# A transformer block with Strassen products: ScalarE's operations of the QKV stages in written order, and the first stage's weight sums moved from GpSimd to VectorE

## The chip, the cores and the metric

The kernel runs on one core of one Trainium2 chip. The metric is the device time of one execution in microseconds (us). All numbers ahead of the result come from one profiled execution of the kernel before the change, and from three timed runs of it.

## The reference

Two sequences of 2048 tokens with 512 features go through one transformer block that a condition vector modulates. All data is float32. Cut to what matters:

```python
mod = silu(condition) @ Wada + bada
sh_a, sc_a, gt_a, sh_m, sc_m, gt_m = split(mod, 6, axis=1)
xn = layernorm(x, g1, be1)
xm = xn * (1 + sc_a) + sh_a
q, k, v = heads(xm @ Wqkv)                 # 16 heads of 32
x = x + gt_a * (causal_softmax(q @ k.T / sqrt(32)) @ v @ Wproj + bproj)
xm = layernorm(x, g2, be2) * (1 + sc_m) + sh_m
x = x + gt_m * (gelu(xm @ W1 + b1) @ W2 + b2)
```

## The kernel before

The program runs, one after the other: the QKV stage of sequence 0 (about 18 to 220 us of the profile), its attention, a projection stage together with the QKV stage of sequence 1 (about 745 to 1005 us), its attention, a projection stage, and the MLP. This change touches the two QKV stages alone.

**A QKV stage** (class `Qkv`) loops over four groups `g` of 512 tokens. A group has six units: four blocks `f` of 128 features of queries and keys (`keys_and_queries`) and two units of values (`values`). Each unit is a 2x2 block product done in Strassen's manner, with seven products instead of eight, on operands that are sums of blocks of the weights (S1, S3, S2, S4 in the table `SUMS`) and sums of blocks of the tokens. The products go into three PSUM banks, a, b and c. The order in a unit is

```python
step("a", A11, True, first, 0, 0), step("b", S1, True, first, 1, 1),
step("a", S2, False, first, 0, 1), step("b", S4, False, last, 0, 1),
step("c", A12, True, last, 0, 0),  step("a", S3, False, last, 1, 1),
step("a", A22, False, direct, 1, 0),
```

A bank that is used again is not cleared: S2 is accumulated on top of A11 in bank a, after ScalarE has copied what A11 left there (`first`, L963 for queries and keys, L1034 for values). `last` is VectorE's addition of a bank to such a copy (L976, L982, L1038). The seventh product, A22, is put off until two products of the next unit have been issued. In the first unit of sequence 0 (`plain`) eight ordinary products replace the seven.

Queries and keys are split into a rounded part `hi`, which ScalarE makes (L968), and the rest `lo`, which VectorE subtracts in groups 0 and 1 and GpSimd in groups 2 and 3 (L970). Both are stored to DRAM by SyncE's queue (L935), and are loaded again in another layout for the attention (L323, L348). There are three `hi` buffers, so a fourth `hi` waits until the first has been stored.

**Slots.** After each product comes a slot (`tick` with its number n, 42 in a group). It holds the work for the next group and other side work: the load of the next x rows (slot 3, L816), the statistics, 1/std and the first two normalised tiles (slot 14: `stats` L216, `inv_std` L222, `normal` L869), transposing and modulating them (slot 18: `norm`, L272), the second two tiles (slots 24 and 28), token sums (L901), in groups 1 to 3 score products `s` whose maxima VectorE takes (L476, L481), and pieces of weight sums for the MLP, which GpSimd adds (L1153) and stores.

**What sets the order.** Each engine runs its instructions in the order of its own queue and waits at the head of it. An instruction wrapped in `act(...)` (or a matmul, in `mm(...)`) keeps its written place among the others so wrapped on its engine. The place of all others is chosen by a scheduler when the program is built, by its own estimate of when they can run. DMA issues are in such queues too, most of them in SyncE's. Before the change, of the ScalarE operations in the QKV stages, none of those of L222, L272, L869, L963, L968, L1009 and L1034 is wrapped.

**Weight sums.** A weight sum is one elementwise addition or subtraction of two blocks in SBUF. For queries and keys each of the four sums of a feature block is 128x256 elements (`weight_sum`, L841), for values 128x512 (`value_weight_sums`, L846). In the first stage GpSimd makes all twenty of them: blocks 1, 2 and 3 and the values in a row ahead of the stage, and block 0 in slot 7 (block 0 of group 0 is `plain` and needs none).

Of the kernel before, what the change touches and what calls it, by code (L numbers as in the profile page):

```python
# [17 lines left out]
P = 128  # L18
# [9 lines left out]
def dit_block_kernel(  # L28
# [177 lines left out]
    def act(ins):  # L206

        return tc.keep_in_program_order(ins)
# [10 lines left out]
        nc.vector.bn_aggr(mv[:, n, :], st)  # L219

    def inv_std(mv, rstd, shift, lo, hi):
        nc.scalar.activation(rstd[:, lo:hi], mv[:, lo:hi, 1], AF.Sqrt, bias=eps)  # L222
        nc.vector.reciprocal(rstd[:, lo:hi], rstd[:, lo:hi])
        nc.vector.scalar_tensor_tensor(
            shift[:, lo:hi], mv[:, lo:hi, 0], -1.0, rstd[:, lo:hi], ALU.mult, ALU.mult
        )
# [7 lines left out]
    def transposed(pool_, psum, xts, n0, mv, rstd, a, c, b, dst, xns=None, share=False):  # L234

        count = len(xts)
        per = 512 // (count * P)  # L240
        by_act = xns is not None
        xns = xns or []
        for t, xt in enumerate(xts):
            if by_act:
                continue
            xn = pool_.tile([P, D], F32, tag="xn", name="xn", bufs=3)
            n = n0 + t
            nc.vector.tensor_scalar(
                xn, xt, mv[:, n, 0:1], rstd[:, n : n + 1], ALU.subtract, ALU.mult
            )  # L250
            xns.append(xn)
        banks = []
        for cc in range(0, C, per):
            ps = psum.tile([P, per, count * P], F32, tag="mm", name="ps_xt")
            for ci in range(per):
                for t in range(count):
                    transpose(
                        ps[:, ci, t * P : (t + 1) * P],
                        xns[t][:, (cc + ci) * P : (cc + ci + 1) * P],
                    )  # L260
            banks.append(ps)

        def modulate(chunks=range(C)):
            for k in chunks:
                src = banks[k // per][:, k % per, :]
                if k % 2 == 0 and (share or not by_act):
                    nc.vector.tensor_scalar(
                        dst[:, k, :], src,
                        a[:, k, b : b + 1], c[:, k, b : b + 1], ALU.mult, ALU.add,
                    )  # L270
                else:
                    nc.scalar.activation(  # L272
                        dst[:, k, :], src, AF.Identity,
                        bias=c[:, k, b : b + 1], scale=a[:, k, b : b + 1],
                    )

        return modulate
# [518 lines left out]
    class Qkv:  # L796
# [43 lines left out]
            w = self.w  # L840
            act(engine.tensor_tensor(w[:, n, :, f], w[:, x, :, f], w[:, y, :, f], op))  # L841

        def value_weight_sums(self):
            w = self.wv
            for n, x, y, op in SUMS:
                act(nc.gpsimd.tensor_tensor(w[:, n], w[:, x], w[:, y], op))  # L846

        def stats(self, g, t, keep=False):

# [5 lines left out]
        def normal(self, g, j, early=False):  # L855

            b = self.row.b
            if j == 0 and g > b:
                for t in range(MTT):
                    self.stats(g, t)  # L860
            for t in (2 * j, 2 * j + 1):
                n, xt = b * NT + g * MTT + t, self.xts[g][t]
                if early:
                    nc.vector.tensor_scalar(
                        xt, xt, mv1[:, n, 0:1], rstd1[:, n : n + 1],
                        ALU.subtract, ALU.mult,
                    )
                else:
                    nc.scalar.activation(  # L869
                        xt, xt, AF.Identity,  # L870
                        bias=shift1[:, n : n + 1], scale=rstd1[:, n : n + 1],
                    )

        def norm(self, g, j, share=False):
# [70 lines left out]
        def keys_and_queries(self, g, f, hp):  # L945

            ops = self.operands(g)
            los = [self.lo_tile(hp) for _ in range(2)]

            def part(i, j):  # L950
                return los[i].bitcast(F32)[:, j * HALF_T : (j + 1) * HALF_T]

            def product(ps, n, new):
                for k in range(HK):
                    mm(
                        ps, self.w[:, n, k, f * P : (f + 1) * P], ops[n][:, k],
                        start=new and k == 0, stop=k == HK - 1,
                        skip_group_check=not new,
                    )

            def first(ps, i, j):
                scale = HD**-0.5 if i == 0 else 1.0
                nc.scalar.activation(part(i, j), ps, AF.Copy, scale=scale)  # L963

            def split(i):
                hi, lo = self.hi_tile(hp), los[i]
                d = lo.bitcast(F32)
                nc.scalar.copy(hi, d)  # L968
                engine = nc.vector if g < 2 else nc.gpsimd
                engine.tensor_tensor(lo, d, hi.bitcast(F32), ALU.subtract)  # L970
                self.stored(g, f, i, (hi, lo))

            def last(ps, i, j):
                d = part(i, j)
                if i == 0:
                    nc.vector.scalar_tensor_tensor(  # L976
                        d, ps, HD**-0.5, d, ALU.mult, ALU.add
                    )
                    if j == 0:
                        split(0)  # L980
                else:
                    nc.vector.tensor_tensor(d, d, ps, ALU.add)  # L982

            def direct(ps, i, j):
                first(ps, i, j)
                split(1)

            return self.unit(product, first, last, direct)

        def plain(self, g, f, hp):  # L990


            xmT, steps = self.xmT[g], []
            for which in range(2):
                box = []
                for k in range(C):
                    def run(which=which, k=k, box=box):
                        if k == 0:
                            box.append(self.psum.tile([P, MT], F32, tag="mm", name="ps_qk"))
                        n = BASE[2 * which + k // HK][0]  # L1000
                        mm(
                            box[0], self.w[:, n, k % HK, f * P : (f + 1) * P], xmT[:, k, :],
                            start=k == 0, stop=k == C - 1,
                        )
                        if k < C - 1:
                            return
                        hi, lo = self.hi_tile(hp), self.lo_tile(hp)
                        scale = HD**-0.5 if which == 0 else 1.0
                        nc.scalar.activation(hi, box[0], AF.Copy, scale=scale)  # L1009
                        nc.vector.scalar_tensor_tensor(  # L1010
                            lo, box[0], scale, hi.bitcast(F32), ALU.mult, ALU.subtract
                        )
                        self.stored(g, f, which, (hi, lo))
                    steps.append(run)
            return steps

        def values(self, g, t):

            ops, vv = self.operands(g), self.row.vv

            def part(i, j):
                w = D // 2
                return vv[:, g * MTT + 2 * j + t, i * w : (i + 1) * w]

            def product(ps, n, new):
                for k in range(HK):
                    mm(
                        ps, ops[n][:, k, t * P : (t + 1) * P], self.wv[:, n, k],
                        start=new and k == 0, stop=k == HK - 1,
                        skip_group_check=not new,  # L1030
                    )

            def first(ps, i, j):
                nc.scalar.copy(part(i, j), ps)  # L1034

            def last(ps, i, j):
                d = part(i, j)
                nc.vector.tensor_tensor(d, d, ps, ALU.add)  # L1038

            return self.unit(product, first, last, first)  # L1040
# [221 lines left out]
    with pool("wada") as wp, pool("qkv0") as qp, pool("hl0") as hp, pool(  # L1262
# [110 lines left out]
                modulate((k, k + 1))  # L1373
        for n in (S1, S2, A22):
            qkv.token_sum(0, n)
        for f in (1, 2, 3):
            for k in range(4):
                qkv.weight_sum(nc.gpsimd, k, slice(f * P, (f + 1) * P))
        act(nc.vector.tensor_copy(pick, pickc.unsqueeze(3).to_broadcast([P, 2, B, P])))

        def also(g, n):

            if (g, n) == (0, 7):
                for k in range(4):
                    qkv.weight_sum(nc.gpsimd, k, slice(0, P))
            pieces.tick()
            if g == 0 and n == 24:
                load_wada(2, 5)
# [6 lines left out]
                else:  # L1395
                    scale_shift(a2, c2, r_g2, r_be2, 3, 4)

        qkv.value_weight_sums()
        pieces = Pieces()
        spare_k = [row.key_room(q) for q in (2, 3)]  # L1400
        w1p, w2p = HK * P, 7 * P
# [32 lines left out]
    with pool("qkv1") as qp, pool("ps_qkv1", bufs=6, space=PSUM) as ps_mm:  # L1434
# [24 lines left out]
        project_phase(past, ps_mm, between)  # L1459

        def also(g, n):
            if (g, n) == (0, 10):
                qkv.value_weight_sums()
            pieces.tick()

        with pool("hl1") as hp:
# [563 lines left out]
```

## Time and profile before

| | us |
|---|---|
| median of 3 runs (2363.38 to 2366.47) | 2365.2 |
| the profiled execution, its own time | 2364.18 |
| its span in the profile | 2362.5 |
| TensorE (PE) busy in the span | 2316.3 (98%) |
| VectorE (DVE) busy | 1437.2 (61%) |
| ScalarE (ACT) busy | 1005.3 (43%) |
| GpSimd (POOL) busy | 1117.3 (47%) |
| first QKV stage, 18.9 to 240 us: PE busy of 221.1 us | 203.8, mean granted clock 0.95 |
| projection and second QKV stage, 745 to 1010 us: PE busy of 265 us | 258.1, clock 1.00 |
| attention of sequence 0, 240 to 745 us: PE busy of 505 us | 501.1, clock 1.00 |

How to read the profile: PEld is TensorE's loading of weights, which runs beside its products. A name such as ACT L963 is an engine and the kernel's line. In a timeline a row gives the start, the busy time, the engine, the line, the operation, the tiles that it writes and reads with their shapes, the number of like instructions that were merged, and in brackets the idle time of the engine before it with what ended that. "SPq" and "POOLq" are DMA issues in a queue. "PEclk" is the share of TensorE's clock that the chip granted. A wait for several things is put down to the one that came last by the profile's reckoning.

### The profile page before, as it was taken

The page shows a single profiled execution, that of the slowest core. Times are in us where ns is not written, and L with a number is a line of the kernel's source. Part 1 is how long each engine was busy: PE and PEld are TensorE (multiplying, and loading weights), DVE is VectorE, ACT ScalarE, POOL GpSimd, SP SyncE. Part 2 cuts the span into 40 slices and gives each one's busy share as a digit, 9 for nine tenths or more (in the row PEclk, how much of TensorE's full clock was granted, in tenths as well). Part 3 has the DMA queues.
Part 4 walks back from the last instruction along what each step waited for, and adds up shares of the span by engine and source line. Part 5 has one row for each costly group of instructions (what it writes and reads, how often), then busy time and mean ns, then how long its engine had stood idle before and what let it go on. Part 6 is the DMA issues. An engine that isn't in the chain of part 4 may idle for free.

```text
span 2362.5 us, 34358 instructions
## 1 busy us (share of the span) xinstructions
PE 2316.3 (98%) x12067; PEld 1409.6 (60%) x12067; DVE 1437.2 (61%) x2964; ACT 1005.3 (43%) x1948; POOL 1117.3 (47%) x1261
## 2 busy tenths in 40 slices
PE   7999999999999999999999999999999999999998
PEld 5777555555554488855555555444585486487477
DVE  5567666666665666776666666653473374365356
ACT  3333555555556144355555555603322322332320
POOL 4343997878884593179887997460000000000000
PEclk9999999999999999999999999999999999999999
DMA  8887233231132787442323113273254254353433
GB/s 249 270 260 221 50 77 72 71 83 46 57 127 82 261 297 250 143 92 59 82 64 99 32 48 123 78 252 108 93 170 149 91 179 143 116 168 127 136 123 130
DMA packets 160518, 311.64 MB, mean 132 GB/s; under 512 B 16544, under 2 KB 48844, under 8 KB 158552
## 3 DMA queue, kind: packets, MB, share of 16 engines
q1 hardware_dynamic: 155488, 285.53, 39.6%
q0 software_dynamic: 4480, 23.36, 2.6%
q8 instruction: 95, 1.56, 0.3%
q14 instruction: 79, 0.65, 0.1%
q10 hardware_dynamic: 376, 0.55, 0.1%
HBM read 229.95 MB, written 87.29 MB: 134 GB/s over the span
## 4 chain that ended last, share of the span: by engine, by line
PE 90%; DVE 3%; DMA 2%; POOL 2%; issue 1%; ACT 1%; SPq 0%; POOLq 0%; DVEq 0%; ACTq 0%
PE ps_a L204 24%; PE st L204 20%; PE ps_b L204 12%; PE o L204 11%; PE s L204 10%; PE ps_c L204 6%; PE sm L204 4%; PE ps_o L204 2%; PE ps_xt L212 1%; DVE mx L481 1%; POOL ee L634 1%; DVE junk L476 1%; PE ps_o L212 1%; DMA x1d<-xt 0%; DMA x<-in_x_dram 0%
## 5 line engine op out<-in xcount | busy, mean ns | idle before, releaser
L606 ACT ACTIVATE e<-st 128x512 f32<-128x512 f32 (+1 forms) x1152 | 573.9, 579 | 429.7 <-PE st L204 358.0
L634 POOL TENSOR_TENSOR ee<-ee,e 128x512 f32<-128x512 f32 x424 | 529.1, 1286 | 4.4 <-ACT e L606 4.1
L481 DVE TENSOR_REDUCE mx<-s 128x1 f32<-128x512 f32 x604 | 407.6, 687 | 196.3 <-PE s L204 195.0
L204 PE MATMUL s<-kst,qst 128*128 128x512 f32 (+3 forms) x1032 | 418.5, 409 | 11.0 <-DVE mx L481 7.1
L204 PE MATMUL st<-qst,kst 128*128 128x512 f32 (+3 forms) x1280 | 409.4, 387 | 0.0
L204 PE MATMUL ps_a<-sum,w 128*128 128x256 f32 (+1 forms) x1088 | 346.6, 454 | 0.0
L204 PE MATMUL o<-e,vv 128*32 128x512 f32 (+3 forms) x2560 | 300.5, 538 | 1.9 <-POOL e L612 1.9
L204 PEld LDWEIGHTS st<-qst,kst 128*128 128x128 f32 x1280 | 227.4, 188 | 94.2 <-issue 62.0
L476 DVE CUSTOM_DVE_ANT_0 junk<-s,causal 128x512 bf16<-128x512 f32 (+3 forms) x428 | 208.7, 488 | 108.1 <-PE s L204 100.0
L204 PEld LDWEIGHTS ps_a<-sum,w 128*128 128x128 f32 x1088 | 206.3, 190 | 109.8 <-issue 91.4
L204 PEld LDWEIGHTS s<-kst,qst 128*128 128x128 f32 x1032 | 194.7, 189 | 124.1 <-DVE mx L481 59.3
L634 POOL TENSOR_TENSOR ee<-e 128x512 f32<-128x512 f32 x168 | 210.4, 1286 | 103.1 <-ACT e L606 99.3
L612 POOL TENSOR_SCALAR_AFFINE_SELECT e<-e 128x128 f32<-128x128 f32 (+1 forms) x384 | 122.1, 353 | 83.8 <-ACT e L606 81.0
L204 PE MATMUL st<-fold,sel 32*128 32x512 f32 (+1 forms) x1152 | 148.5, 480 | 0.4
L1609 DVE TENSOR_TENSOR h<-c,ps_b 128x512 f32<-128x512 f32 x32 | 22.0, 689 | 202.0 <-PE ps_b L204 202.0
L204 PEld LDWEIGHTS st<-fold,sel 32*128 32x128 f32 x1152 | 59.2, 181 | 143.2 <-ACT e L606 86.6
L204 PEld LDWEIGHTS o<-e,vv 128*32 128x32 f32 x2560 | 61.5, 108 | 101.5 <-issue 79.4
L204 PE MATMUL ps_b<-sum,w 128*128 128x256 f32 (+1 forms) x384 | 120.6, 450 | 0.0
L1783 ACT ACTIVATE h<-h,cols 128x512 f32<-128x512 f32 x96 | 69.3, 722 | 120.4 <-DVE h L1609 120.4
L481 DVE TENSOR_REDUCE mx<-st 128x1 f32<-128x512 f32 x164 | 112.7, 687 | 4.2 <-PE st L204 1.8
L970 POOL TENSOR_TENSOR lo<-lo,hi 128x512 fp32r<-128x512 f32 x32 | 40.6, 1271 | 147.6 <-ACT hi L968 147.5
L204 PEld LDWEIGHTS ps_b<-sum,w 128*128 128x128 f32 x384 | 73.0, 190 | 37.2 <-issue 30.6
(208 smaller groups left out, 3117.6 us busy)
## 6 DMA issues: line engine op xcount, KB each, us to landing
qst<-q SPq DMA_DIRECT2D x128, 256.0 KB
kst<-k SPq DMA_DIRECT2D x128, 256.0 KB
w<-w1d SPq DMA_DIRECT2D x32, 896.0 KB
w<-w2d SPq DMA_DIRECT2D x28, 1024.0 KB
w<-w2d SPq DMA_DIRECT2D x28, 768.0 KB
q<-hi SPq DMA_DIRECT2D x32, 256.0 KB
q<-lo SPq DMA_DIRECT2D x32, 256.0 KB
k<-hi SPq DMA_DIRECT2D x32, 256.0 KB
```

The costliest lines, as they stand in the source:

```text
L204: return tc.keep_in_program_order(nc.tensor.matmul(*args, **kw))
L212: return tc.keep_in_program_order(nc.tensor.transpose(dst, src, ident[:n, :n]))
L476: nc.vector.tensor_tensor_reduce(junk[:, :w], s[:, :w], causal[:, QB - w :], 1.0, MASKED, ALU.add, ALU.max, m,)
L481: nc.vector.tensor_reduce(m, s[:, :w], axis=AX.X, op=ALU.max)
L606: act(nc.scalar.activation(e[:, :w], sts[h][:, :w], AF.Exp))
L612: nc.gpsimd.affine_select(d, d, pattern=[[0, len(tiles)], [1, P]], compare_op=ALU.is_ge, fill=0.0, base=0, channel_multiplier=-1,)
L634: act(engine.tensor_tensor(dst, x, y, ALU.add))
L970: engine.tensor_tensor(lo, d, hi.bitcast(F32), ALU.subtract)
L1609: act(nc.vector.tensor_tensor(dst, x, y, ALU.add))
L1783: nc.scalar.activation(d, ps, AF.Gelu, bias=col(r_b1 + half * HF + f, 1))
```

## The change

All ScalarE operations of the QKV stages are wrapped in `act`, so that they stand in ScalarE's queue in the order in which the code issues them. In the first stage VectorE makes the weight sums: the four of block 1 ahead of the stage, and then one in every other slot from slot 7 on: block 2 in slots 7 to 13, block 3 in 15 to 21, the values in 23 to 29, block 0 in 31 to 37. In the second stage the four value sums stay on GpSimd, but are issued one each in slots 10 to 13 instead of four in slot 10.

```diff
 def inv_std(mv, rstd, shift, lo, hi):
-    nc.scalar.activation(rstd[:, lo:hi], mv[:, lo:hi, 1], AF.Sqrt, bias=eps)
+    act(nc.scalar.activation(rstd[:, lo:hi], mv[:, lo:hi, 1], AF.Sqrt, bias=eps))
...
 # in the same way: modulate (L272), normal (L869), first and split of
 # keys_and_queries (L963, L968), plain (L1009), first of values (L1034)
...
-    def value_weight_sums(self):
+    def value_weight_sum(self, engine, k):
+        n, x, y, op = SUMS[k]
         w = self.wv
-        for n, x, y, op in SUMS:
-            act(nc.gpsimd.tensor_tensor(w[:, n], w[:, x], w[:, y], op))
+        act(engine.tensor_tensor(w[:, n], w[:, x], w[:, y], op))
...
-    for f in (1, 2, 3):
-        for k in range(4):
-            qkv.weight_sum(nc.gpsimd, k, slice(f * P, (f + 1) * P))
+    for k in range(4):
+        qkv.weight_sum(nc.vector, k, slice(P, 2 * P))
...
     def also(g, n):
-        if (g, n) == (0, 7):
-            for k in range(4):
-                qkv.weight_sum(nc.gpsimd, k, slice(0, P))
+        if g == 0 and 7 <= n < 39 and n % 2:
+            part, k = (n - 7) // 8, (n - 7) % 8 // 2
+            if part == 2:
+                qkv.value_weight_sum(nc.vector, k)
+            else:
+                f = (2, 3, None, 0)[part]
+                qkv.weight_sum(nc.vector, k, slice(f * P, (f + 1) * P))
...
-    qkv.value_weight_sums()
...
     def also(g, n):                      # second stage
-        if (g, n) == (0, 10):
-            qkv.value_weight_sums()
+        if g == 0 and 10 <= n < 14:
+            qkv.value_weight_sum(nc.gpsimd, n - 10)
```

More of the change, by code (lines that the diff above doesn't have):

```diff
@@ L271, in modulate @@
                 else:
-                    nc.scalar.activation(
-                        dst[:, k, :], src, AF.Identity,
-                        bias=c[:, k, b : b + 1], scale=a[:, k, b : b + 1],
+                    act(
+                        nc.scalar.activation(
+                            dst[:, k, :], src, AF.Identity,
+                            bias=c[:, k, b : b + 1], scale=a[:, k, b : b + 1],
+                        )
                     )
@@ L868, in normal @@
                 else:
-                    nc.scalar.activation(
-                        xt, xt, AF.Identity,
-                        bias=shift1[:, n : n + 1], scale=rstd1[:, n : n + 1],
+                    act(
+                        nc.scalar.activation(
+                            xt, xt, AF.Identity,
+                            bias=shift1[:, n : n + 1], scale=rstd1[:, n : n + 1],
+                        )
                     )
@@ L962, in first @@
                 scale = HD**-0.5 if i == 0 else 1.0
-                nc.scalar.activation(part(i, j), ps, AF.Copy, scale=scale)
+                act(nc.scalar.activation(part(i, j), ps, AF.Copy, scale=scale))
             def split(i):
@@ L967, in split @@
                 d = lo.bitcast(F32)
-                nc.scalar.copy(hi, d)
+                act(nc.scalar.copy(hi, d))
                 engine = nc.vector if g < 2 else nc.gpsimd
@@ L1008, in run @@
                         scale = HD**-0.5 if which == 0 else 1.0
-                        nc.scalar.activation(hi, box[0], AF.Copy, scale=scale)
+                        act(nc.scalar.activation(hi, box[0], AF.Copy, scale=scale))
                         nc.vector.scalar_tensor_tensor(
@@ L1033, in first @@
             def first(ps, i, j):
-                nc.scalar.copy(part(i, j), ps)
+                act(nc.scalar.copy(part(i, j), ps))
             def last(ps, i, j):
```

## The prediction

> **What bounds the kernel now.** I read the table by windows first, to see where TensorE is not busy. The change touches the two QKV stages only, and the built programs show TensorE's order to be the same before and after; so what can be won is TensorE's idle time there, and its time at a low clock. Columns: window, length, busy time of PE, PEld, DVE, ACT, POOL, then granted clock, DMA share, GB/s.
>
> ```profile
> 20.00:40.00 20.00, 11.52 (x32) 6.93 (x31) 13.49 (x17) 6.93 (x12) 18.46 (x23) 0.77 0.66 210
> 40.00:60.00 20.00, 20.00 (x100) 17.63 (x100) 6.40 (x13) 10.53 (x26) 3.72 (x3) 0.98 0.87 238
> 80.00:100.00 20.00, 15.43 (x62) 12.75 (x61) 9.91 (x30) 8.12 (x18) 3.90 (x5) 0.83 0.97 343
> 140.00:144.00 4.00, 1.80 (x7) 1.03 (x6) 2.53 (x11) 2.62 (x6) 1.25 (x1) 0.91 1.04 356
> 144.00:148.00 4.00, 3.86 (x16) 3.50 (x17) 1.23 (x3) 3.45 (x8) 3.20 (x5) 0.66 0.80 225
> ```
>
> There are three holes, and after each the clock is low for a while. The timeline says what made them. The first:
>
> ```profile
> 26.07 0.60 ACT L1009 ACTIVATE hi<-ps_qk 128x512 fp32r<-128x512 f32 x1 [2.84 <-PE ps_qk L204]
> 26.68 1.28 ACT L222 ACT_TABLE_LOAD   x1
> 30.41 5.37 POOL L846 TENSOR_TENSOR wv<-wv 128x512 f32<-128x512 f32 x4
> 30.69 3.96 DVE L901 TENSOR_TENSOR xmT<-xmT 128x512 f32<-128x512 f32 x1
> 35.57 0.30 ACT L222 ACTIVATE rstd<-mv,eps 128x4 f32<-128x4 f32 x1 [7.61 <-DVE mv L219]
> 35.78 0.36 ACT L963 ACTIVATE lo<-ps_a 128x256 f32<-128x256 f32 x1
> 36.24 2.05 PE L204 MATMUL ps_a<-t,wqk 128*128 128x256 f32 x4 [8.48 <-POOL wv L846]
> ```
>
> PE ended S1 of block 1 at 27.76 and could not accumulate S2 before ScalarE had copied bank a. ScalarE's scheduler-made order put the next group's 1/std (L222) first; that waited for VectorE's statistics, and VectorE was in a token sum that took 3.96 us beside GpSimd's weight sums. The profile names POOL as PE's releaser, but the weight sums that S2 needs ended by 26; the copy that ends at 36.14 is the one. The second hole:
>
> ```profile
> 70.19 0.61 ACT L968 CAST hi<-lo 128x512 fp32r<-128x512 f32 x1
> 70.83 0.32 SPq L935 DMA_DIRECT2D k<-hi  x1
> 71.92 2.58 DVE L970 TENSOR_TENSOR lo<-lo,hi 128x512 fp32r<-128x512 f32 x1
> 77.60 4.35 SPq L816 DMA_DIRECT2D x<-in_x_dram  x4
> 85.33 0.69 DVE L216 BATCH_NORM_STATS2 stat<-x 128x6 f32<-128x512 f32 x1 [6.67 <-DMA x<-in_x_dram]
> 89.55 3.78 PE L204 MATMUL ps_a<-t,wqk 128*128 128x256 f32 x8 [1.87 <-DVE lo L982]
> ```
>
> The last `hi` of group 0 was made at 70.19, though its input had been ready since 59.58: it stood behind the copies of the values. Its store, the `lo` behind it and the x rows of group 2, in SyncE's one queue, all came late; VectorE stood at the statistics until 85.33, with score maxima and additions behind it, and PE was idle for 2.70 + 1.87 = 4.57 us. The third hole (141.62 to 144.14) has the same cause with x of group 3: 1.81 + 0.23 us before `ps_xt`, 0.29 before.
>
> The low clock: PE worked at half rate from 36.24 to 40.9 (2.3 us lost), from 89.55 to 95.5 (3.0) and over 3.4 us from 143.3 (1.7), read from windows of 4 us (88 to 92: 0.58, 92 to 96: 0.56). So the holes cost 10.8, 7.6 and 4.0 us.
>
> **The change, part by part.** The reckoning goes by the queues of the changed program with the durations of this trace, and is made against the profiled execution (2364.18 us: its span of 2362.5 and 1.7 around it), which is 1.0 below the median.
>
> *A, the first hole: +7.0.* ScalarE's queue is now: copies of A11, S1, S2 and the split of block 1, copies of A11 and S1 of block 2, and only then table load, 1/std and two normalised tiles. VectorE has the three token sums (0.69 each, with GpSimd silent) and the weight sums. A sum of 128x256 from SBUF is not in the trace for VectorE: half of the 0.69 of 128x512 is 0.35, the 128x256 additions from PSUM (L976) take 0.42; I take 0.35. So the sum for S2 is there by 27.2 and ScalarE's copy by 27.3, and PE's third product starts near 27.6, not at 36.24. From 25.87 to the first product of the values PE has 20 products of 0.86 and one transposing of 0.87: it would be there at 44.0; before it was at 55.0. But new waits come in. VectorE's queue from 25.3 on (token sum, 4 weight sums, two `lo` of `plain`, the `pick` copy, a token sum, 2 sums, two statistics, three additions) is some 8.7 us long and reaches the addition (L982) that A22 waits for at 34.0, where PE wants it at 32.8: 1.4 with the signal. The block-2 sum for S2 follows that: 0.7. The table load (1.28), 1/std (0.30) and two tiles (1.52) are now between copies that PE waits for: transposing 0.7 late, S3 another 0.5, S2 of block 3 behind four modulations (1.93) 0.7. Sum 4.0, so 11.0 - 4.0 = 7.0. Bounds: 4 if VectorE's stretch is as slow as beside GpSimd, 9.5 if half of the waits don't come.
>
> *B, a new wait: -2.4.* The fourth value sum stands in VectorE's queue behind `lo` of block 3's keys, and that behind ScalarE's `hi`. Before, from the transposing at 56.75 to the end of the copy at 59.58 were 2.83 us (four modulations in front); then come 0.62 (`hi`), 0.69 (`lo`) and 0.69 (the sum), with signals 5.0 in all. PE reaches S4 of the values 2.6 after the transposing (59.35): 2.4 idle. Bounds: 0, and -6 where VectorE's two operations each meet a GpSimd addition (the `lo` beside them took 0.97 and 2.58, not 0.69) and the clock falls: here 2.3 us of idle in three pieces were followed by
>
> ```profile
> 144.14 1.76 PE L212 MATMUL ps_xt<-ident,x 128*128 128x128 f32 x7 [0.23 <-ACT x L869]
> ```
>
> at half rate, worth 1.7. [...]
>
> *C, the second hole: +6.6.* The last `hi` of group 0 now follows its copy at once, so `k<-lo` goes out at about 54 and the x rows follow from 57 to 61, landing by 66; VectorE reaches the statistics at 64, and A22 of group 1, the first to need what is behind them, comes at 74. But SyncE's queue is changed there: the eight W1 loads (`kst`, `qst`, L1132), before at 109 and 120, now stand ahead of group 1's first `q<-hi` store, and wait until GpSimd's `w2d` stores have read those buffers. GpSimd's additions started at 56.28, after W2 loads that are some 6 us earlier now, and had issued the ones waited for 19.5 later: about 70, landed by 76 (6.0 in the DMA view); four loads and five of Wada at 0.48, and the store goes at 80.5, landing at 83.5. ScalarE wants that `hi` buffer near 81.3: about 1 us for PE. Bounds: 0 and 7.6.
>
> *D, the third: +3.4* of 4.0; the x rows of group 3 again follow a `hi` that no longer waits behind other copies. Bounds 0 and 4.0.
>
> *E, the second stage: +1.5.* Its idle pieces between 823 and 926 are 0.67, 0.24, 0.37, 0.35, 0.40, 1.22 and 0.38; the last four come with statistics and 1/std, and half of the 3.6 should go. The value sums, now between GpSimd's other additions, end some 2 us later, by 848; S4 needs them at 851. Bounds -2 and 3.6.
>
> *F, written order elsewhere: -1.0.* In the later groups 1/std and two tiles (0.30, 0.5 for VectorE's reciprocal, 1.52) stand ahead of a copy, but PE has three products and two score products there (3.4): hidden. I put 1.0 for places where it isn't; bounds 0 and -4. `modulate` is used by the MLP too; ScalarE's order there stays.
>
> *G, the moved work itself:* 16 x 0.35 + 4 x 0.69 = 8.4 us more for VectorE, which is busy for 6.4 of 20 us in the window from 40; hidden, but for the waits above. GpSimd loses 12.1 + 5.3 us that nobody else waited for. [...]
>
> Sum: 7.0 - 2.4 + 6.6 + 3.4 + 1.5 - 1.0 = 15.1; 2364.2 - 15.1 + 1.0 = 2350.
>
> **Rivals.** *R1, the x rows come no earlier.* DMA is full in these stretches (share 0.97 from 80 to 100), so a load that is issued earlier may land as late, or the SyncE queue holds it. Then C and D give nothing: 15.1 - 10.0 = 5.1 us faster, 2360. Against it: the load was late mostly by its issue, 18 us after the copy that it depends on, and took 7.7 to land. *R2, VectorE becomes the limit of group 0*: sums as slow as GpSimd's row (0.78 and 1.34) add 9 us to it and A and B together give nothing: 10.5 faster, 2355. *R3, slower: the store behind the W1 loads.* Each us that SyncE's queue holds `q<-hi` past the 81.3 at which ScalarE wants the buffer stops ScalarE, and so PE, by as much, and the clock goes with it (3.0). [...] With 20 us and 3.0 for the clock 15.1 - 23 = -8: 2373. *R4, nothing:* the holes come back one queue on, within 4.7 us of the time before.
>
> **How the numbers follow.** Forecast as reckoned, 2342 to 2355: 0.56, its likeliest value 2350. R2, up to 2357: 0.14. R1, 2357 to 2361: 0.12. R4: 0.08. R3: 0.08. Faster still: 0.02. A measurement of this kernel can tell about 0.2%, 4.7 us. Faster takes the forecast, what is faster still, R2 and most of R1: 0.83; same 0.09 (R4 and the rest of R1); slower 0.08. The range, 2342 to 2361, takes all bounds of A to D but the worst together, and leaves out R3 and most of R4.
>
> **What would show it.** In the changed profile: third product of block 1 within 1 us of the second, PEclk 1.0 from 20 to 50; a PE wait of 2 to 3 us in the first values unit, with VectorE's sum as releaser; x of group 2 issued 15 us or more before 77; no wait of VectorE's statistics for x over 3 us; ScalarE waiting for the DMA of `q<-hi` by 0 to 4 us. I am wrong if one of the three holes stays at its size, or if PE waits over 5 us for ScalarE or VectorE anywhere in the stages.

## The result, and the profile after it

The changed kernel takes 2368.55 us (median of 20 runs, 2363.75 to 2373.96), the kernel before 2364.16 us in the same rounds (20 runs, 2356.75 to 2366.68). The ratio is 1.0024, with a 95% interval of 1.0016 to 1.0032: slower by 4.4 us, a small difference, but one that the interval tells from none. The forecast was 2350 us, 15 us faster.

The profiled execution of the changed kernel was its fastest of the twenty (2363.75 us, span 2361.7). So its waits are on the small side; two more executions of the unaltered kernel were profiled below.

The table by windows again, after the change (window, length, busy time of PE, PEld, DVE, ACT, POOL, then granted clock, DMA share, GB/s):

```profile
20.00:40.00 20.00, 19.41 (x77) 13.74 (x76) 12.97 (x33) 8.12 (x16) 0.00 (x0) 0.98 0.91 277
40.00:60.00 20.00, 16.27 (x71) 13.48 (x70) 13.84 (x20) 10.32 (x23) 13.66 (x14) 0.91 1.02 320
80.00:100.00 20.00, 16.35 (x78) 13.61 (x78) 10.32 (x29) 9.95 (x21) 4.21 (x6) 0.99 0.95 326
140.00:144.00 4.00, 4.00 (x21) 3.42 (x20) 2.66 (x8) 1.62 (x4) 3.89 (x5) 1.00 0.96 297
...
840.00:860.00 20.00, 14.76 (x68) 12.40 (x67) 11.32 (x19) 5.83 (x15) 19.78 (x25) 0.93 0.99 357
```

The first and the third hole are closed (PE 19.41 instead of 11.52, and 4.00 of 4.00; the work of the third hole now lies earlier, but TensorE has no idle piece over 0.25 us anywhere from 98.2 to 210 us). The hole at 80 to 100 is only smaller, 40 to 60 has a new one, and so has the second stage, where before TensorE had been busy throughout:

```profile
840.00:860.00 20.00, 20.00 (x99) 17.68 (x98) 11.63 (x13) 9.60 (x23) 19.90 (x25) 1.00 0.96 332
```

That is a row of the kernel before. What happens there after the change, in the timeline of all engines:

```profile
846.42 2.55 SPq L818 DMA_DIRECT2D x<-in_x_dram  x4
...
851.39 0.69 DVE L216 BATCH_NORM_STATS2 stat<-x 128x6 f32<-128x512 f32 x1 [2.96 <-DMA x<-in_x_dram]
...
852.00 2.63 DVE L905 TENSOR_TENSOR xmT<-xmT 128x512 f32<-128x512 f32 x1
...
852.81 10.36 POOL L1157 TENSOR_TENSOR vv<-vv 128x512 f32<-128x512 f32 x9
...
854.55 1.75 DVE L905 TENSOR_TENSOR t<-xmT,t 128x512 f32<-128x512 f32 x1
...
858.21 0.40 DVE L1042 TENSOR_TENSOR vv<-vv,ps_a 128x256 f32<-128x256 f32 x1
...
858.67 2.08 PE L204 MATMUL ps_a<-wv,t 128*128 128x256 f32 x4 [4.92 <-DVE vv L1042]
```

VectorE's queue now has the first statistics of the next group's x ahead of two token sums and three value additions, the last of which TensorE waits for. They stand 2.96 us for x, which was issued 4.97 us before; two more statistics (0.65 and 0.68 us) stand among the value additions. The token sums take 2.63 and 1.75 us instead of 0.69, beside GpSimd's additions, but that is not new: before the change three of them took 1.57 to 1.75 us in the same place, and TensorE did not wait. TensorE waits 4.92 us and then works at half clock until 864. Before the change the same rows were these, from its timeline:

```profile
859.09 1.75 DVE L901 TENSOR_TENSOR t<-xmT,t 128x512 f32<-128x512 f32 x1
...
861.43 0.41 DVE L1038 TENSOR_TENSOR vv<-vv,ps_a 128x256 f32<-128x256 f32 x1
...
865.45 1.82 SPq L816 DMA_DIRECT2D x<-in_x_dram  x4
...
868.82 0.69 DVE L216 BATCH_NORM_STATS2 stat<-x 128x6 f32<-128x512 f32 x1
```

x was issued 19 us later, behind a late store of `k<-lo`. Of these 19 us 8.7 are the stage's own later start; counted from its first product, x came at 43.6 us before and comes at 33.2 after, 10 us earlier. The scheduler had put the statistics behind the value additions, where they waited for nothing. **The written order brought x forward, and in the same program VectorE's statistics stand in front of work that TensorE waits for.** That the scheduler moved them because x comes earlier is an inference; what it reckoned is not on record.

To compare kernels, each stage is measured in its profile as TensorE sees it: the first from the first `ps_qk` product to the last `ps_a` product of the values, the second from the first `ps_a` product to the last. "us" is the median of the runs; the lengths are of one execution (the fastest of its runs for the changed kernel's first profile, first_values_early, repaired_x_free and hi_four, the slowest for repaired).

| kernel | us | first stage | second stage |
|---|---|---|---|
| before | 2364.2 | 201.6 | 177.5 |
| after, first profile | 2368.5 | 193.6 | 185.6 |
| after_two, after_three | one run each: 2368.4, 2369.4 | 194.3, 196.8 | 189.4, 185.7 |
| first_stage | 2357.0 | 194.0 | 177.8 |
| second_stage | 2372.0 | 201.3 | 186.3 |
| order_only | 2367.9 | 192.4 | 187.5 |
| sums_only | 2356.2 | 193.4 | 178.5 |
| stats_spread | 2362.1 | 196.0 | 180.6 |
| x_free | 2367.1 | 195.3 | 186.5 |
| first_values_early | 2351.1 | 188.9 | 175.4 |
| sums_values_early | 2357.7 | 193.8 | 176.9 |
| repaired | 2356.8 | 189.0 | 181.8 |
| repaired_x_free | 2355.6 | 189.0 | 180.7 |
| best | 2353.0 | 191.6 | 176.3 |
| hi_four | 2347.1 | 183.8 | 175.3 |

### The profile page after: what moved, and what is told of

It is laid out like the page before. It is cut to its first block, busy times and chain, and to the rows that moved or that the text cites. A ratio compares the mean times of both kernels' runs of the same rounds, so it can differ in the third digit from the quotient of the medians.

```text
span 2361.7 us, 34347 instructions
## 1 busy us (share of the span) xinstructions
PE 2315.8 (98%) x12067; PEld 1410.5 (60%) x12067; DVE 1446.2 (61%) x2984; ACT 1005.6 (43%) x1948; POOL 1103.5 (47%) x1241
## 4 chain that ended last, share of the span: by engine, by line
PE 88%; DMA 4%; DVE 3%; POOL 2%; issue 1%; ACT 1%; SPq 0%; DVEq 0%; POOLq 0%; ACTq 0%
PE ps_a L204 23%; PE st L204 20%; PE ps_b L204 11%; PE o L204 11%; PE s L204 10%; PE ps_c L204 6%; PE sm L204 4%; PE ps_o L204 2%; DMA q<-hi 1%; PE ps_xt L212 1%; POOL ee L636 1%; DVE mx L483 1%; DMA k<-lo 1%; DMA x<-in_x_dram 1%; PE ps_o L212 1%
```

## The experiments

In the diffs `ordered` is the changed kernel's `act` for ScalarE, but with a switch: with `written[0]` false it leaves the place to the scheduler, as before the change. It and other edits shift line numbers by 2 to 5.

**Which stage wins and which loses: first_stage and second_stage.**

```diff
+    written = [True]            # second_stage: False here and True below
+    def ordered(ins):
+        return tc.keep_in_program_order(ins) if written[0] else ins
...
+    written[0] = False
     past, row = row, Row(1)
```

In first_stage the second stage's value sums are again four in slot 10; in second_stage the first stage's sums are again on GpSimd.

> The whole change in the first sequence's QKV stage; the second one's as before the change (scheduler's order on ScalarE, value sums in a row). Theory: the first stage wins about 8 us and the second loses it again. In the profiled run after the change TensorE was 8.8 us ahead of before at 211 us, 0.8 of that from before its stage began, and 0.7 us ahead at 1006 us. So here 2364 - 8 = 2356 us, ratio 0.9966, with the waits of the first stage as after the change (3.6 us at 51, 1.2 at 67, 2.7 at 96). Rival: the profiled run was the fastest of twenty, and the median loses its 5 us in the first stage, by low clock after those waits; then 2361 to 2365 us, ratio 0.9985 to 1.0005.

> The other half alone: ScalarE's written order and the spaced value sums in the second sequence's QKV stage, the first stage as before the change. Theory: TensorE waits some 5 us for VectorE about 40 us into the stage, where statistics stand ahead of the value additions and wait for x, then 1.5 and 1.8 us more, and half clock after the first: 8 us or more, so 2372 to 2377 us, ratio 1.0034 to 1.0055. Rival: the second stage lost only what any earlier arrival there gives back; then 2363 to 2367 us, ratio 0.9995 to 1.001.

Measured: first_stage 2357.0 us, ratio 0.997 (0.9961 to 0.9979); second_stage 2372.0 us, ratio 1.0038 (1.0026 to 1.005). The theory holds in both, the rivals in neither: the change wins 7 us in the first stage and loses 8 in the second. The lengths say the same: each half moves its own stage, by 7.6 and 8.8 us, and leaves the other within 0.3.

**Which part of the change: order_only and sums_only.**

```diff
 # order_only: after, but as before the change
-    for k in range(4):
-        qkv.weight_sum(nc.vector, k, slice(P, 2 * P))
+    for f in (1, 2, 3):
+        for k in range(4):
+            qkv.weight_sum(nc.gpsimd, k, slice(f * P, (f + 1) * P))
...      # and so for block 0 (slot 7) and the values (in a row, both stages)
 # sums_only: after, with
+    written = [False]           # for both stages
```

> ScalarE's written order in both stages; all weight sums in a row on GpSimd as before the change. Theory: the three old holes came from ScalarE's order, so they close here too; the new wait of 3.6 us for VectorE's value sum, with the half clock behind it (about 2), isn't there; in the first hole VectorE's token sum stays slow beside GpSimd, at most 3 us of TensorE's time. Second stage as after: 8 lost. Sum: 8 + 5.6 - 3 - 8 = 2.6 faster: 2357 to 2366 us, ratio 0.997 to 1.001. Rival: the first hole came from the sums on GpSimd (the profile's releaser) and stays at 8 us: 2368 to 2374 us, ratio 1.0015 to 1.004.

> The moved weight sums alone; ScalarE in the scheduler's order in both stages. Theory: the second and third hole stay (waits of 4.6 and 2.3 us), the first shrinks as far as GpSimd's silence frees VectorE (from 8.5 to some 4 us), and the wait for the fourth value sum comes on top (2 to 4 us): within 3 us of the time before, 2361 to 2367 us, ratio 0.9987 to 1.0013. Rival: the sums carry the first stage's gain; then 2354 to 2358 us, ratio 0.996 to 0.9975.

Measured: order_only 2367.9 us, ratio 1.0017 (1.0009 to 1.0025), which lies between the two ranges by its time and just inside the rival's by its ratio, so its profile decides. The first hole is down to 2.77 us, where the rival had it stay at 8, and the first stage is as short as with the whole change: the rival's cause is out. But the second stage is as long too, so its loss needs only the written order, not the spaced sums. With sums_only the theory failed and the rival held: 2356.2 us, ratio 0.997 (0.9958 to 0.9981). Either half alone shortens the first stage by 8 to 9 us and both together by 8 to 5. What holds TensorE in the first hole is a chain of two links, and breaking one is enough. With the written order alone VectorE's token sum is as slow as ever, but ScalarE no longer stands behind it (timeline of order_only, all engines):

```profile
29.86 3.97 DVE L905 TENSOR_TENSOR xmT<-xmT 128x512 f32<-128x512 f32 x1
...
33.98 1.97 PE L204 MATMUL ps_a<-xmT,wqk 128*128 128x256 f32 x8 [2.77 <-DVE mv L219]
```

A wait of 2.77 us instead of 8.48. With the sums alone the token sum takes 0.69 us and the first hole is gone, but the new wait for the fourth value sum is the largest of all these kernels (waits of PE in sums_only, 19 to 215 us: us in total, times, longest):

```profile
PE ps_b L204 <- DVE wv L853: 6.2, 1, 6.2
```

**What the second stage waits for: stats_spread and x_free.**

```diff
 # stats_spread, in tick() of the second stage; normal() no longer calls stats there
+    if self.row.b and g and 10 <= n < 14:
+        self.stats(g + 1, n - 10, True)      # True: pinned behind what is issued before
 # x_free: after, with 1/std (L222) and the x tiles (L872) as before
-        act(nc.scalar.activation(rstd[:, lo:hi], mv[:, lo:hi, 1], AF.Sqrt, bias=eps))
+        nc.scalar.activation(rstd[:, lo:hi], mv[:, lo:hi, 1], AF.Sqrt, bias=eps)
...      # and so for the x tiles
```

> The change, with one edit more: in the second stage the statistics of groups 2 and 3 are issued one in each of slots 10 to 13 and pinned there, instead of wherever the scheduler puts them (it had put the first ahead of the token sums and value additions that TensorE waits for). Theory: the second stage's loss is VectorE standing at the statistics for x; then the wait of 4.9 us (6.7 in the run with the second half alone), the half clock after it (2) and that of 1.8 go: 2368.5 - 8 = 2360 us, ratio 0.997 to 0.9995. Rival: the loss is the written order itself, copies behind normalised x tiles and splits that wait for a store; then at most 3 us come back: 2365 to 2368 us, ratio 1.0005 to 1.0015.

> The change without the written order for 1/std and the normalised x tiles (both stages); copies, splits and modulation stay in written order. Theory: the statistics still stand ahead in the second stage, since it is the earlier stores that let x be issued early; the wait of 4.9 to 6.7 us stays, only the waits of 0.9 to 1.9 us behind the x tiles go: 2364 to 2370 us, ratio 1.000 to 1.0025. Rival: the x tiles in written order are what costs: 2356 to 2361 us, ratio 0.9965 to 0.9985.

Measured: stats_spread 2362.1 us, ratio 0.999 (0.9978 to 1.0001), 2 us beyond the theory's time, within its range of ratios and outside the rival's. VectorE's statistics wait for x nowhere in its second stage, and that stage is 180.6 us long, 5.0 to 8.8 less than in the three profiles of the changed kernel. x is issued as early there as in the changed kernel, 33.2 us into the stage, but the statistics stand behind the additions (timeline of stats_spread):

```profile
858.39 0.41 DVE L1042 TENSOR_TENSOR vv<-vv,ps_a 128x256 f32<-128x256 f32 x1
...
868.20 0.68 DVE L216 BATCH_NORM_STATS2 stat<-x 128x6 f32<-128x512 f32 x1
```

x_free 2367.1 us, ratio 1.0013 (1.0004 to 1.0023), in the range of its theory: with the x tiles free the statistics still stand ahead, and the stage is as long as ever (186.5). The one wait of 4.9 to 6.7 us that the theory kept is not there, though: TensorE waits 2.3 us at 856 and 3.2 us at 905 behind statistics, and 2.2 us at 893 for a ScalarE copy. So it is not the place of the x tiles that costs, and giving the statistics another place takes most of the loss away.

**The fourth value sum: first_values_early and sums_values_early.**

```diff
-                if part == 2:
-                    qkv.value_weight_sum(nc.vector, k)
+            if g == 0 and 16 <= n < 24 and n % 2 == 0:
+                qkv.value_weight_sum(nc.vector, n // 2 - 8)
```

> The change in the first stage alone (2357.0 us), with the four value sums in slots 16, 18, 20 and 22 instead of 23 to 29. Theory: the wait of 4.1 us for the fourth value sum goes, with the time at half clock behind it (2.2): 2351 us, ratio 0.9935 to 0.9955. Rival: what TensorE gains there it gives back at the next wait, for ScalarE's split that waits for a store in the full DMA queues near 96 us; then 2355 to 2358 us, ratio 0.996 to 0.9975.

> The moved sums alone, ScalarE in the scheduler's order (2356.2 us), with the value sums in slots 16 to 22. Theory: its wait of 6.2 us for the fourth value sum goes, with the half clock behind it (2.2): 2348 us, ratio 0.992 to 0.9945. Rival: given back at the statistics that wait for x near 90 us; 2353 to 2356 us, ratio 0.9955 to 0.9965.

Measured: first_values_early 2351.1 us, ratio 0.9948 (0.9934 to 0.9962), the number of the theory; the wait of 4.1 us is gone, and one of 2.6 us at 62 has come. sums_values_early 2357.7 us, ratio 0.9972 (0.9962 to 0.9982): no faster than sums_only. Its wait of 6.2 is gone as well, but TensorE waits 4.3 and 1.8 us at 76 to 83 for VectorE, which stands at the statistics for x (waits in sums_values_early, 70 to 90 us):

```profile
DVE stat L221 <- DMA x<-in_x_dram: 7.4, 1, 7.4
```

So the rival's cause held there, with a time just above its range: without the written order the old second hole takes the time back. With the value sums early the written order is worth 6.5 us (2357.7 against 2351.1; a part may be the spacing of the second stage's value sums, in which the two differ as well).

**Both repairs: repaired, and repaired_x_free.** The first is the changed kernel with the two edits of stats_spread and first_values_early; the second also leaves 1/std and the x tiles of the second stage to the scheduler.

> The whole change with both edits: statistics of the second stage spread over slots 10 to 13, value sums of the first stage in slots 16 to 22. Theory: the two losses are separate, so 2368.5 - 8 - 6 = 2354 us, ratio 0.9945 to 0.997. Rival: written order still loses in the second stage, 2359 to 2362 us, ratio 0.998 to 0.999.

> The whole change with statistics spread and value sums early (2356.8 us), and the second stage's 1/std and x tiles left to the scheduler. Theory: what is left of the second stage's loss (181.8 us long in that profile, 177.5 before) are the waits behind 1/std and the x tiles in written order, 0.8 to 1.5 us each: 2 to 4 us back, 2353 to 2355 us, ratio 0.9945 to 0.996. Rival: it is VectorE, with the statistics now ahead of the additions that TensorE waits for (1.0, 0.9 and 2.0 us); then no change, 2356 to 2358 us, ratio 0.9965 to 0.9975.

Measured: 2356.8 us, ratio 0.9971 (0.9959 to 0.9982), and 2355.6 us, ratio 0.9965 (0.9952 to 0.9978). repaired lies 3 us above the theory's sum and below the rival's range: its first stage keeps the whole gain, and its second stays 4.3 us longer than before (in the slowest of its six runs). With the x tiles free 1.1 us of that go, between the two expectations and less than the interval can tell; its waits there are for VectorE's additions behind the spread statistics (1.4), for ScalarE's copies (1.5 and 0.5) and for score maxima (1.3). Which of them is worth what was not separated: the last 3 to 4 us of the second stage stay open.

**What is left in the first stage: best and hi_four.**

```diff
 # best: first_values_early, with block 0's four sums
-                f = (2, 3, None, 0)[part]      # block 0 in slots 31 to 37
...
+            if g == 0 and 24 <= n < 28:
+                qkv.weight_sum(nc.vector, n - 24, slice(0, P))
 # hi_four: best, with
-            return hp.tile([P, MT], F32R, tag="hi", name="hi", bufs=3)
+            return hp.tile([P, MT], F32R, tag="hi", name="hi", bufs=4)
...          # and lo: bufs=6 -> 5
```

> The change in the first stage alone with the value sums in slots 16 to 22 (2351.1 us), and the four sums of block 0 in slots 24 to 27 instead of 31 to 37, which is ahead of GpSimd's additions. Theory: VectorE spent 3.0 us on three of them between 54.9 and 59.2, beside GpSimd, and came late to the value additions by 2.6 us; without them the wait and the half clock behind it (1.7) go: 2347 us, ratio 0.9915 to 0.994. Rival: the token sums beside GpSimd (one took 3.4) keep VectorE late; 2349 to 2352 us, ratio 0.994 to 0.9955.

> The kernel with the first stage's order and the sums moved early (2353.0 us), with four buffers for hi instead of three and five for lo instead of six. Theory: ScalarE's splits near 80 and 89 us wait for a hi buffer whose store q<-hi took 8.3 and 5.2 us from issue to landing in full DMA queues; with a fourth buffer the waits of 1.6 and 2.7 us and the half clock after them (1.7) go: 2347 us, ratio 0.9915 to 0.994. Rival: the lo buffers, one fewer and stored through the same queue, or x, are as late: no change, 2351 to 2355 us, ratio 0.9945 to 0.9965.

Measured: best 2353.0 us, ratio 0.9948 (0.9936 to 0.9961): no gain. The wait at 62 us went as the theory said, but two waits of ScalarE for the store of `q<-hi` took its place, a third outcome that neither had (waits of ScalarE in best, 20 to 215 us):

```profile
ACT hi L977 <- DMA q<-hi: 7.6, 2, 4.2
```

hi_four 2347.1 us, ratio 0.9927 (0.9913 to 0.9941), the number of its theory: that wait is gone from its profile, TensorE's longest wait in the two stages is 1.8 us, and the clock is full in both of them from 23.2 us on (0.92 from 20 to 40, 1.00 from 40 to 100, 0.999 over the whole profile). It is 17 us faster than the kernel before and 21 faster than the change. With the buffers some places in SyncE's and VectorE's queues moved too, so not all of its 6 us against best need be the buffer's, and the intervals of the two ratios overlap a little.

**Where the median's last microseconds are: after_two and after_three**, the changed kernel unaltered.

> The changed kernel unaltered, for a second profile: the first was of the fastest of twenty executions (2363.8, median 2368.5). If the missing 5 us lie in the second stage, its wait near 854 is 6 to 7 us here, as in the run with the second half alone, and the stage loses 12 instead of 8; if they lie in low clock, there are one or two more stretches at half clock after waits of 1.5 to 3 us.

> The same once more, for the spread between executions: the same two explanations, the same numbers.

Measured: 2368.4 and 2369.4 us. Both explanations hold in part. TensorE's waits behind the statistics are 5.5 and 6.9 us instead of 4.9 (waits of PE in after_three, 815 to 1010 us), but the stage loses 12 us in after_two alone:

```profile
PE ps_a L204 <- DVE vv L1042: 7.5, 2, 6.9
```

Each shows half rate in a place where the first profile has the full clock (1.00 from 780 to 820 and from 880 to 920). In after_two a wait of 3.1 us at 896, for a ScalarE copy, is followed by it (four products in 2.07 us), and the second stage is 11.9 longer than before; in after_three it falls into the projection ahead of the second stage (eight transposings in 1.86 us from 792.13, in 1.04 from 778.49; from the first stage to the second it takes 2.5 us more) and the first stage is 3 us longer than in the first profile. The mean of the three executions, 2367.2 us, is 3.0 above the profiled execution of before: the first stage 6.7 shorter, the second 9.4 longer, 1.0 lost between them, and 0.9 won ahead of the first stage.

## Why the prediction was wrong

**A, the first hole (+7.0): right in mechanism, and near in size by some luck.** The products of the values begin at 46.2 us instead of 55.0, 0.8 of it from an earlier start: 8.0. The new waits, put at 4.0, took 1.7 from the first product of block 1 on; the products ahead of it, for which the step had no term, took 1.4 longer, at half clock until 21.0 as the clock stood in this execution. A weight sum of 128x256 took VectorE 0.42 us alone, not 0.35. And the step credits the whole to the two edits together, while order_only and sums_only show that either would have done.

**B, the fourth value sum (-2.4): mechanism right, size wrong.** The sum stands where the step put it and TensorE waits for it (timeline of the changed kernel):

```profile
49.58 1.76 DVE L848 TENSOR_TENSOR wv<-wv 128x512 f32<-128x512 f32 x1
...
51.48 1.54 DVE L974 TENSOR_TENSOR lo<-lo,hi 128x512 fp32r<-128x512 f32 x1
...
52.94 1.21 DVE L848 TENSOR_TENSOR wv<-wv 128x512 f32<-128x512 f32 x1
...
54.29 1.27 PE L204 MATMUL ps_b<-wv,xmT 128*128 128x256 f32 x4 [3.58 <-DVE wv L848]
```

The term took 0.69 us for each of the two operations; they took 1.54 and 1.21, and the third sum ahead of them 1.76, each beside a GpSimd addition. The sum put nothing for the clock behind a wait of 2.4 us, which was the author's estimate and is not shown; here 3.4 us at half clock followed (55.09 to 58.50, 1.7 lost), and it cost 5.3, near the bound of 6. The bound was the better value: step C has GpSimd's additions start 6 us earlier than 56.28, and so lie there.

**C, the second hole (+6.6): the hole went, a new wait came.** x of group 2 was issued at 55.95 instead of 77.60 and the statistics no longer wait for it. But the store of `q<-hi` costs more than the 1 us allowed. In the changed kernel's timeline (ScalarE and TensorE):

```profile
97.26 0.62 ACT L972 CAST hi<-lo 128x512 fp32r<-128x512 f32 x1 [3.83 <-DMA q<-hi]
...
98.22 1.13 PE L204 MATMUL ps_a<-xmT,wqk 128*128 128x256 f32 x4 [2.71 <-ACT lo L967]
```

and in its chain (start, us, what):

```profile
82.99 9.71 DMA k<-lo
93.11 4.06 DMA q<-hi
```

The eight W1 loads were out of SyncE's queue by 75, as reckoned; what held the later `q<-hi` store were the attention's key loads (`kst<-k`), which read from DRAM what `k<-hi` and `k<-lo` store. SyncE's queue stood 6.7 us for the landing of the first and 0.9 for that of the second, which took 9.7 us with the DMA engines busy (share 0.95 in the row from 80). This is rival R3's wait with another load in front, 2.7 us of it instead of 20. With 0.9 us behind the x tiles and 1.7 of half clock it cost 5.3; another 1.2 went at 67, where VectorE's sums of block 0 ran beside GpSimd. So C gave about 1 of 6.6. best and hi_four confirm the wait: there it came back, and went with a fourth buffer.

**D, the third hole (+3.4): right**, 4.0.

**A to D together** were to give 14.6 and gave 8.0, 7.3 and 4.8 in the three profiles.

**E, the second stage (+1.5, bounds -2 and 3.6): the step that failed.** It lost 8.1, 11.9 and 8.2 us. The step looked at TensorE's idle pieces of before, 3.6 us in all, and asked only which of them would go. It did not carry C's own mechanism over: that `hi` and its stores come early, and so x, and that readers of x whose place the scheduler chooses come early too. It followed VectorE's queue, with the statistics in it, in the first stage only, and named no new wait in the second. In their place the runs showed TensorE's wait of 4.9, 5.5 and 6.9 us for the value additions behind the statistics; with half the time to the end of the half clock after it that is 7.6, 7.6 and 8.8 us. second_stage and stats_spread put the loss there: 8 us for the half alone, 6 of them back with the statistics in another place.

A second wait adds to it, of a size that changes between executions: step C's, once more. Near 900 us ScalarE's split stands for the store of `q<-hi`, with a copy behind it that TensorE waits for: 0.6, 3.1 and 2.3 us in the three profiles, 2.0 in second_stage (timeline of after_two):

```profile
898.25 0.62 ACT L972 CAST hi<-lo 128x512 fp32r<-128x512 f32 x1 [4.59 <-DMA q<-hi]
...
899.19 2.07 PE L204 MATMUL ps_a<-wv,xmT 128*128 128x256 f32 x4 [3.07 <-ACT vv L1038]
```

In stats_spread TensorE has no such wait, so not all of its 6 us need be the statistics'. No run separates the two: none has a fourth `hi` buffer together with the written order in the second stage.

**F (-1.0): too small, within its bounds.** TensorE waits 0.88 us (at 85) and 1.45 (at 876) behind 1/std and x tiles; both are in the losses of C and E above. **G: hidden**, apart from B and the 1.2 us at 67. Its eight last sums took 10.3 us instead of the 4.4 that they take alone: 5.9 more.

**The rivals.** R1 and R2 did not come: x did land earlier, and VectorE's extra work cost only B. R3's wait came, at the size above. No run shows the 20 us in R3's sum: in the changed kernel SyncE's queue stood 6.7 and 0.9 us for the stores, and ScalarE 3.8 for its buffer. R4, the holes coming back one queue on within 4.7 us of the time before, had 0.08 and is nearest to what happened: 4.4 us slower by the medians. By the prediction's own sign of being wrong the forecast fails, too: TensorE waited more than 5 us for VectorE in two of the three profiles, and 4.92 in the first.

## What to carry to other kernels

Written order on one engine moves the others: follow what its earlier results release (stores, then loads, then the readers of those loads) and look where the scheduler has put those readers, in every stage that runs the same code. A reader that is hoisted above work that others wait for, and whose data lands late, turns an earlier load into a loss; pin it where its data is sure to be there. When two edits aim at one wait, try each alone before their gains are added: here either one took 8 us off the first stage, and the second added nothing, until the new wait that the moved sums had brought was removed; then it added 5 (193.8 against 188.9 us).

## What the runs showed of the hardware

**The half clock came in whole steps, and not by the length of the wait alone.** In the clock records of the kernel before and of the changed kernel's first profile the stretches at half clock inside the stages last 3.4, 6.8 or 10.2 us (30.64 to 40.88, 88.67 to 95.49 and 143.28 to 146.69 before; 55.09 to 58.50, 99.46 to 102.87 and 857.22 to 864.05 after), and those at full clock between them are 14, 14, 12 and 221 times as long as the shortest. A wait of 1.9 us (stats_spread at 85, clock 0.57 from 88 to 92) was followed by 3.4 us at half clock, and one of 2.1 (sums_only at 93) by products at half rate (four in 1.69 us, 1.03 before it). One of 3.6 us (the changed kernel, to 54.29) was followed by 3.4 us, and one of 3.7 (stats_spread at 52, clock 1.00 from 52 to 88) by none. So a wait of 2 to 4 us had no fixed price here: from 0 to 1.7 us more.

What the clock did went with how the idle time lay to the steps. The changes of the clock in each of the two records lie on one grid of 3.41 us. Cut along it, from 20 to 1008 us, six steps at full clock are followed by half clock: in them TensorE idled 2.88, 3.09 and 1.95 us before the change, 2.62, 2.17 and 3.41 after it. In no other step at full clock did it idle more than 1.01 us before and 1.57 after. After a step at half clock another followed where TensorE idled 0.89 us or more in it, and full clock where it idled 0.39 or less. The wait of 3.7 us in stats_spread lies across the steps that its clock of 0.57 from 88 to 92, and 0.71 and 0.86 from 100 to 108, gives: about 2.0 in one and 1.7 in the next, with full clock after both. So near 2 us the runs show both. The ends of products are modelled in the profile, so these figures are good to some 0.1 us.

The runs do not show that this is what spreads their times (9.9 us between the fastest and the slowest of twenty before the change, 10.2 after it): among five runs each it was 3.7 us for hi_four, with no half clock from 23.2 us on in its profile, and 1.5 for best, with half rate at 95.5 (four products in 1.65 us, 0.86 from 99.81).

**VectorE beside GpSimd.** A token sum of 128x512, 0.69 us alone, took 2.63 in the changed kernel at 852 and 3.97 in order_only; a weight sum of 128x256, 0.42 alone, 2.92 in the changed kernel at 59 us.
